# Two of four norm tiles on VectorE: a state-space layer and its experts on one core

## The chip, the cores and the metric

One core of a Trainium2 chip runs the whole program in one launch. Its engines work side by side, each through its own list of instructions in order: TensorE (PE) for matmuls, VectorE (DVE), ScalarE (ACT) and GpSimd (POOL) for elementwise work, SyncE (SP) for starting transfers. The metric is the device time of one launch in microseconds; lower is better.

## The reference, cut to what matters

The input is x, 16 sequences of 256 tokens with 128 features. All norms here are plain: mean and variance over the 128 features of a token.

```python
def layer(x):                       # _L0_attn_ref
    x1 = x + mamba(norm(x) * ln1_g + ln1_b)
    h  = norm(x1) * ln2_g + ln2_b                   # second norm of the layer
    return x1 + relu(h @ ffn_w1.T + b1) @ ffn_w2.T + b2

def experts(x):                     # _L0_ffn_ref, 8 experts, all of them dense
    return sum(silu(x @ Wg[e]) * (x @ Wu[e]) @ Wd[e] for e in range(8))

x = norm(x + layer(x))              # this norm stands ahead of the experts
out = norm(x + experts(x))
```

Inside `mamba` are a projection, a causal convolution over four tokens, a SiLU, a scan over the 256 tokens with 16 states for each of 256 channels, a gate and an output projection. The norms carry 1e-5 beside the variance.

## The kernel before, in words

The 4096 tokens are worked on in 8 groups of 512 (two sequences each). A tile of activations is 128 partitions by 512 numbers, seen as four blocks of 128x128: in a norm, the 128 partitions are tokens, and each of the four blocks has its own column of means and variances.

A group passes through these stages, each a Python generator that is advanced step by step:

- `stage_a` normalises the input (norm "a"), transposes it on TensorE (`pxn`), projects it (`pi`), runs the convolution (`stage_conv`: one ScalarE instruction, three VectorE instructions on `hc`, for each of two halves), and makes the scan's inputs (`pd`, `dbc`, `pv`, `dt`, `u`).
- The scan has 32 steps for a group: `decay` (ScalarE, an exponential into `dA`, in PSUM), `inject` (GpSimd, `dBx`), `step` (VectorE's scan instruction, then the product `hC` with C on VectorE, or on GpSimd with the scan's result in `hS`), `add_state` (a sum over states, on GpSimd into `y` or on TensorE into `py`).
- `stage_c` follows a group's scan: the output projection `po`, the sum `x1`, norm "b" into `x1h`, its transpose `ph`, the small feed-forward part (`pf`, `r`, `pff`), the sum `res`, norm "c" into `x2`, its transpose `px`, and the copy `x2T`, with which the experts can begin.
- `up`, `across` and `down` are the experts' matmuls (`pg`, `pu`, `acc`), with a SiLU on ScalarE and a product on VectorE between; `stage_e` ends a group with norm "e" and the store.

Stages of different groups are interleaved: while group 0 is in `stage_c`, group 1 is in its scan and group 2 in `stage_a`; the experts of group 0 then run beside the scan of group 1. The order is written out by hand, in the strings `PRE`, `START` and `TURN`: each letter is one step of one stage (A for `stage_a` and the convolution, C for `stage_c`, s for a scan step on VectorE, p for one with its product on GpSimd, and so on). A step issues its instructions to their engines there and then, and no engine reorders them. Ahead of the first experts, the letter m puts transposes of a constant (`busy`) on TensorE.

A norm has two functions. `norm_stats` (lines 268 to 286) issues four statistics and four aggregations on VectorE, then two small VectorE instructions on 128x4 numbers (`nm`, the negated mean, line 279, and `ve`, the variance plus 1e-5, line 281), then two on GpSimd: the power -1/2 of `ve` (`rs`, line 283) and the product of `nm` and `rs` (`nb`, line 285). `norm_apply` (line 288) then issues four ScalarE instructions, one for each block, that scale by `rs` and add `nb`. `stage_c` calls it twice: at line 582 for `x1h` and at line 630 for `x2`.

Three things around it matter for what follows. The scan's B and C rows are loaded by SyncE, four steps at a time, into two buffers each; a load waits until the last reader of its buffer is done, and what stands behind it on SyncE's queue waits too. The load of the next group's input, `xt` (line 209), is on the same queue. And `dA` has three PSUM banks, `hC` and `dBx` have six buffers each.

Of the kernel before, what the change touches and what calls it, by code (L numbers as in the profile page):

```python
# [8 lines left out]
FP = mybir.dt.float32  # L9
AF = mybir.ActivationFunctionType  # L10
ALU = mybir.AluOpType

P = 128
# [9 lines left out]
NTT = TB // P  # L23
# [15 lines left out]
EPS = 1e-5  # L39
# [90 lines left out]
def kernel(  # L130
# [25 lines left out]
    nc = tc.nc  # L156
# [11 lines left out]
    small = ctx.enter_context(tc.tile_pool(name="small", bufs=4))  # L168
# [17 lines left out]
    def wide(tag, name, bufs, w=TB):  # L186
        return act.tile([P, TB], FP, tag=tag, bufs=bufs, name=name)[:, :w]

    def wides(tag, name, bufs, n, w):
        t = act.tile([P, n * TB], FP, tag=tag, bufs=bufs, name=name)  # L190
        return t[:, : n * w].rearrange("p (n w) -> p n w", n=n)

    def blocks(tag, name, bufs, n):
        return act.tile([P, NTT, DM], FP, tag=tag, bufs=bufs, name=name)[:, :n, :]
# [70 lines left out]
    def as4(t):  # L265
        return t.rearrange("p (c d) -> p c d", d=DM)

    def norm_stats(src, name):

        n = src.shape[1]  # L270
        st = small.tile([P, NTT, 6], FP, tag="st", name=f"st_{name}")
        mv = small.tile([P, NTT, 2], FP, tag="mv", name=f"mv_{name}")
        for c in range(n):
            nc.vector.bn_stats(st[:, c, :], src[:, c, :])
        for c in range(n):
            nc.vector.bn_aggr(mv[:, c, :], st[:, c, :])

        nm = small.tile([P, NTT], FP, tag="nm", name=f"nm_{name}")
        nc.vector.tensor_scalar(nm[:, :n], mv[:, :n, 0], -1.0, None, ALU.mult)
        ve = small.tile([P, NTT], FP, tag="ve", name=f"ve_{name}")  # L280
        nc.vector.tensor_scalar(ve[:, :n], mv[:, :n, 1], EPS, None, ALU.add)  # L281
        rs = small.tile([P, NTT], FP, tag="rs", name=f"rs_{name}")
        nc.gpsimd.tensor_tensor(rs[:, :n], ve[:, :n], mhalf[:, :n], ALU.pow)  # L283
        nb = small.tile([P, NTT], FP, tag="nb", name=f"nb_{name}")
        nc.gpsimd.tensor_tensor(nb[:, :n], nm[:, :n], rs[:, :n], ALU.mult)
        return rs[:, :n], nb[:, :n]

    def norm_apply(src, dst, scale):
        rs, nb = scale
        for c in range(src.shape[1]):  # L290
            nc.scalar.activation(  # L291
                dst[:, c, :], src[:, c, :], AF.Identity, bias=nb[:, c : c + 1], scale=rs[:, c : c + 1]
            )

    def transpose(pt, src):

        for c in range(src.shape[1]):
            nc.tensor.transpose(pt[:, bass.ts(c, P)], src[:, c, :], ident)
# [6 lines left out]
    def take(name, w, more=0):  # L305

        while len(held) >= limit[0] + more or not free or len(free) <= HELD[1] * (limit[0] == HELD[1]):
            yield
            yield
        held.add(name)  # L310
        return grab(name, w)

    def done(name):
        held.remove(name)
        give(name)
# [23 lines left out]
    def stage_a(g):  # L339
        xt = x_tiles[g]  # L340
        s = state[g] = {}
        yield
        scale = norm_stats(xt, f"a{g}")
        yield
        yield
        yield
        xh = wide("xh", f"xh{g}", 2, W[g])
        norm_apply(xt, as4(xh), scale)
        yield
        pt = yield from take(f"pxn{g}", W[g])  # L350
# [165 lines left out]
    def add_state(t, on_pe):  # L516
# [18 lines left out]
        if last:  # L535
            assert s["gated"] >= h
            if ("sum", h) in s:
                nc.tensor.matmul(
                    s["sum", h], lhsT=ident, rhs=y, start=False,
                    stop=h == NH - 1 or sums(g, NH - 1)[0] != name, skip_group_check=True,  # L540
                )
                y = s["sum", h]
            if h == 0:
                s["yt"] = wides("yt", f"yt{g}", 1, NH, W[g])

            engine = nc.vector if y is not s["y", h] else nc.gpsimd
            engine.tensor_tensor(s["yt"][:, h, :], y, s["zg"][:, h, :], ALU.mult)  # L547
            if name in owner and (h == NH - 1 or sums(g, NH - 1)[0] != name):
                give(name)
            if h == NH - 1:  # L550
                launch("C", stage_c(g))


    def stage_c(g):
        s = state[g]
        xt = x_tiles[g]
        xtf = xt.rearrange("p c d -> p (c d)")
        yield
        po = yield from take(f"po{g}", W[g])
        for c in range(W[g] // P):  # L560
            for h in range(NH):
                nc.tensor.matmul(  # L562
                    po[:, bass.ts(c, P)], lhsT=s["yt"][:, h, bass.ts(c, P)], rhs=outw[:, h, :],
                    start=(h == 0), stop=(h == NH - 1),
                )
        yield
        yield
        x1 = wide("x1", f"x1{g}", 1, W[g])
        nc.vector.tensor_add(x1, po, xtf)
        done(f"po{g}")  # L570
        scale = norm_stats(as4(x1), f"b{g}")
        yield
        yield

        res = wide("res", f"res{g}", 1, W[g])
        nc.gpsimd.tensor_tensor(res, x1, xtf, ALU.add)
        nc.gpsimd.tensor_tensor(
            as4(res), as4(res), fb2_bc[:, :].unsqueeze(1).to_broadcast([P, W[g] // P, DM]), ALU.add
        )
        yield  # L580
        xh = wide("xh", f"x1h{g}", 2, W[g])
        norm_apply(as4(x1), as4(xh), scale)
        yield
        pt = yield from take(f"ph{g}", W[g])
        transpose(pt, as4(xh))
        yield
        h2 = wide("h2", f"h2{g}", 1, W[g])
        nc.scalar.activation(h2, pt, AF.Identity, bias=b2_sb[:, 0:1], scale=g2_sb[:, 0:1])
        done(f"ph{g}")
        yield  # L590
        r = wides("r", f"r{g}", 1, NF, W[g])
        po = None

        def second(f, start, stop):
            for c in range(W[g] // P):
                nc.tensor.matmul(  # L596
                    po[:, bass.ts(c, P)], lhsT=r[:, f, bass.ts(c, P)], rhs=w2[:, f, :],
                    start=start and c == 0, stop=stop and c == W[g] // P - 1, skip_group_check=True,
                )


        if g == 0:
            po = yield from take(f"pff{g}", W[g])
        for f in range(NF):
            pf = yield from take(f"pf{g}_{f}", W[g])
            nc.tensor.matmul(pf, lhsT=w1[:, bass.ts(f, P)], rhs=h2, start=True, stop=True)  # L606
            if g == 0 and f > 0:
                second(f - 1, f == 1, False)
            yield
            nc.scalar.activation(r[:, f, :], pf, AF.Relu, bias=fb1_sb[:, f : f + 1])  # L610
            done(f"pf{g}_{f}")
            yield
        if g > 0:
            po = yield from take(f"pff{g}", W[g])
            for f in range(NF - 1):
                second(f, f == 0, False)
                if f == 1:
                    yield
                    yield
        second(NF - 1, False, True)  # L620
        yield
        yield
        nc.vector.tensor_add(res, po, res)
        done(f"pff{g}")
        scale = norm_stats(as4(res), f"c{g}")
        yield
        yield
        yield
        x2 = blocks("x2", f"x2{g}", 2, W[g] // P)
        norm_apply(as4(res), x2, scale)  # L630
        yield
        pt = yield from take(f"px{g}", W[g])
        transpose(pt, x2)
        yield
        x2T = wide("x2T", f"x2T{g}", 2, W[g])
        nc.scalar.copy(x2T, pt)
        done(f"px{g}")
        state[g] = dict(x2=x2, x2T=x2T)
        slices.extend((g, n) for n in range(NJ[g]))
        yield  # L640
# [163 lines left out]
    while at["w"] < sum(NJ) or any(running.values()):  # L804
# [3 lines left out]
        g, k = scans[min(at["a"], len(scans) - 1)]  # L808
# [56 lines left out]
```

## Time and profile before

| | us |
|---|---|
| median of 3 runs | 932.52 (931.58 to 932.66) |
| the profiled execution | 932.79 |
| its span, first to last instruction | 931.0 |

| engine | busy, us | share of the span |
|---|---|---|
| TensorE | 880.1 | 95% |
| VectorE | 713.9 | 77% |
| ScalarE | 710.9 | 76% |
| GpSimd | 717.6 | 77% |

| what | when, us |
|---|---|
| scan of group 0 ends, `po` of group 0 | 93.8 |
| norm "b" of group 0, ScalarE's part | 99.79 to 101.44 |
| norm "c" of group 0, ScalarE's part | 120.36 to 122.01 |
| first expert matmul | 123.15 |
| last scan's work on GpSimd | 712.8 |
| last matmul of the experts | 923.1 |

The profile is one execution, recorded by the hardware. A row of its timeline gives the start in us from the beginning of the span, the length in us, the engine, the line, the instruction, what it writes and reads with the shapes, and how many of the same kind are merged in the row. In brackets is the time for which the engine sat idle before it, and what released it. VectorE's, ScalarE's and GpSimd's shares are averages over stretches of very different kinds: all three are nearly full while scans and experts run side by side, up to 713 us, and nearly free behind that, where TensorE works alone.

### The profile page before, as it was taken

The page shows a single profiled execution, that of the slowest core. Times are in us where ns is not written, and L with a number is a line of the kernel's source. Part 1 is how long each engine was busy: PE and PEld are TensorE (multiplying, and loading weights), DVE is VectorE, ACT ScalarE, POOL GpSimd, SP SyncE. Part 2 cuts the span into 40 slices and gives each one's busy share as a digit, 9 for nine tenths or more (in the row PEclk, how much of TensorE's full clock was granted, in tenths as well). Part 3 has the DMA queues.
Part 4 walks back from the last instruction along what each step waited for, and adds up shares of the span by engine and source line. Part 5 has one row for each costly group of instructions (what it writes and reads, how often), then busy time and mean ns, then how long its engine had stood idle before and what let it go on. Part 6 is the DMA issues. An engine that isn't in the chain of part 4 may idle for free. (4 is left out here: it accounts for less than half of the span.)

```text
span 931.0 us, 8901 instructions
## 1 busy us (share of the span) xinstructions
PE 880.1 (95%) x2520; PEld 421.2 (45%) x2520; DVE 713.9 (77%) x1144; ACT 710.9 (76%) x995; POOL 717.6 (77%) x637
## 2 busy tenths in 40 slices
PE   5878797999999999999999999999999999999996
PEld 2333443445444543445344543454344544455564
DVE  5699875676989889988988998988898899723222
ACT  5834588888899799989898889979998889533222
POOL 1699999998999887998799879999799979700000
PEclk9799899999999999999999999999999999999999
DMA  7574321121233222222322223221322222000000
GB/s 203 199 236 136 125 71 68 68 103 58 81 102 111 83 90 61 90 90 102 94 80 90 80 94 101 91 94 54 104 90 92 91 79 90 1 1 11 1 0 12
DMA packets 38417, 79.76 MB, mean 86 GB/s; under 512 B 5968, under 2 KB 19168, under 8 KB 38368
## 3 DMA queue, kind: packets, MB, share of 16 engines
q1 hardware_dynamic: 33744, 76.58, 24.6%
q10 hardware_dynamic: 4624, 2.62, 1.0%
q8 instruction: 20, 0.33, 0.1%
q14 instruction: 29, 0.24, 0.1%
HBM read 76.57 MB, written 2.62 MB: 85 GB/s over the span
## 5 line engine op out<-in xcount | busy, mean ns | idle before, releaser
L497 POOL TENSOR_TENSOR dBx<-B,u 128x512 f32<-128x512 f32 x256 | 320.9, 1278 | 17.6 <-DMA B<-bc 17.6
L505 DVE TENSOR_TENSOR_SCAN dA<-dA,dBx 128x512 f32<-128x512 f32 x229 | 279.8, 1222 | 17.5 <-ACT dA L485 14.8
L534 POOL TENSOR_TENSOR y<-y,hC 128x512 f32<-128x512 f32 x223 | 279.6, 1276 | 0.7 <-DVE hC L508 0.6
L652 PE MATMUL pg<-x2T,wg 128*128 128x512 f32 x512 | 253.7, 597 | 7.5 <-ACT h L654 4.8
L661 PE MATMUL pu<-x2T,wu 128*128 128x512 f32 x512 | 250.5, 594 | 4.7 <-ACT h L654 3.3
L679 PE MATMUL acc<-h,wd 128*128 128x512 f32 (+1 forms) x576 | 251.4, 545 | 0.1
L662 DVE TENSOR_TENSOR h<-pu,h 128x512 f32<-128x512 f32 x256 | 170.8, 684 | 104.4 <-PE pu L661 101.4
L654 ACT ACTIVATE h<-pg 128x512 f32<-128x512 f32 x256 | 147.1, 597 | 113.8 <-PE pg L652 111.9
L485 ACT ACTIVATE dA<-dt,A 128x512 f32<-128x512 f32 x256 | 169.5, 685 | 42.1 <-DVE hC L508 34.8
L508 DVE TENSOR_TENSOR hC<-dA,C 128x512 f32<-128x512 f32 x229 | 158.3, 691 | 19.4 <-POOL y L534 4.4
L679 PEld LDWEIGHTS acc<-h,wd 128*128 128x128 f32 x576 | 107.5, 191 | 110.3 <-issue 100.0
L661 PEld LDWEIGHTS pu<-x2T,wu 128*128 128x128 f32 x512 | 95.7, 190 | 124.6 <-issue 90.2
L652 PEld LDWEIGHTS pg<-x2T,wg 128*128 128x128 f32 x512 | 93.8, 190 | 122.6 <-issue 82.7
L485 ACT ACT_TABLE_LOAD x91 | 116.8, 1283 | 2.4 <-ACT x L291 0.5
L654 ACT ACT_TABLE_LOAD x90 | 115.5, 1283 | 3.3 <-ACT dbc L377 1.8
L283 POOL TENSOR_TENSOR rs_e<-ve_e,mhalf 128x4 f32<-128x4 f32 (+1 forms) x9 | 8.5, 946 | 123.3 <-DVE ve_e L281 123.3
L532 PE MATMUL py<-hC,ident 128*128 128x512 f32 x66 | 39.3, 698 | 11.9 <-DVE hC L508 8.0
L505 DVE TENSOR_TENSOR_SCAN hS<-dA,dBx 128x512 f32<-128x512 f32 x27 | 32.3, 1211 | 13.2 <-POOL hC L508 7.2
L449 DVE SCALAR_TENSOR_TENSOR hc<-pi,cw,hc 128x510 f32<-128x510 f32 (+2 forms) x48 | 35.5, 744 | 5.2 <-ACT hc L442 4.0
L508 POOL TENSOR_TENSOR hC<-hS,C 128x512 f32<-128x512 f32 x27 | 34.4, 1277 | 5.4 <-issue 3.0
L596 PEld LDWEIGHTS pff<-w,r 128*128 128x128 f32 x256 | 31.5, 193 | 9.4 <-issue 6.2
L596 PE MATMUL pff<-w,r 128*128 128x128 f32 x256 | 32.1, 278 | 0.9 <-ACT r L610 0.9
(92 smaller groups left out, 595.9 us busy)
## 6 DMA issues: line engine op xcount, KB each, us to landing
B<-bc SPq DMA_DIRECT2D x63, 512.0 KB, 3.9
C<-bc SPq DMA_DIRECT2D x63, 512.0 KB, 4.3
xt<-in_x_dram SPq DMA_DIRECT2D x8, 256.0 KB, 4.4
wg<-in_Wg_dram SPq DMA_DIRECT2D x8, 256.0 KB, 5.7
wu<-in_Wu_dram SPq DMA_DIRECT2D x8, 256.0 KB, 5.6
wd<-in_Wd_dram SPq DMA_DIRECT2D x8, 256.0 KB, 5.4
out_dram<-x ACTq DMA_DIRECT2D x7, 256.0 KB, 4.1
bc<-dbc ACTq DMA_DIRECT2D x8, 64.0 KB, 2.2
```

Of the source, the lines that this page charges most:

```text
L485: nc.scalar.activation(s["dA", k], s["dt"][:, h, :], AF.Exp, scale=A_sb[:, h, n : n + 1])
L497: nc.gpsimd.tensor_tensor(s["dBx", k], s["B", k // NL][:, n % NC, :], s["u"][:, h, :], ALU.mult)
L505: nc.vector.tensor_tensor_scan(to, dA, s.pop(("dBx", k)), 0.0, ALU.mult, ALU.add)
L508: engine.tensor_tensor(hC, to, s["C", k // NL][:, k // NH % NC, :], ALU.mult)
L532: nc.tensor.matmul(s["sum", h], lhsT=ident, rhs=hC, start=first, stop=False, skip_group_check=True)
L534: nc.gpsimd.tensor_tensor(y, y, hC, ALU.add)
L596: nc.tensor.matmul(po[:, bass.ts(c, P)], lhsT=r[:, f, bass.ts(c, P)], rhs=w2[:, f, :], start=start and c == 0, stop=stop and c == W[g] // ...
L652: nc.tensor.matmul(pg[:, cols], lhsT=wg[:, e, bass.ts(f, P)], rhs=s["x2T"], start=True, stop=True)
L654: nc.scalar.activation(s["h", j], pg, AF.Silu)
L661: nc.tensor.matmul(pu[:, cols], lhsT=wu[:, e, bass.ts(f, P)], rhs=s["x2T"], start=True, stop=True)
L662: nc.vector.tensor_mul(s["h", j], pu, s["h", j])
L679: nc.tensor.matmul(acc, lhsT=wd[:, e, f, :], rhs=h[:, cols][:, bass.ts(part, acc.shape[1])], start=(e == 0 and f == 0), stop=(e == NE - 1 ...
```

## The change

In the two norms of `stage_c`, for group 0 alone, blocks 0 and 1 stay on ScalarE, and blocks 2 and 3 go to VectorE as `tensor_scalar` instructions with two scalars read per partition (multiply by `rs`, add `nb`). Their place in VectorE's order follows from where `stage_c` issues them. For `x1h` they come behind the scan instruction into `hS` at 98.28 us and ahead of the one at 99.42 us; for `x2`, behind the six convolution instructions of group 2 at 118.85 us and ahead of the scan at 123.28 us. GpSimd's, TensorE's and SyncE's orders are what they were. In every norm of all groups, `ve` is now issued ahead of `nm`.

```diff
         for c in range(n):
             nc.vector.bn_aggr(mv[:, c, :], st[:, c, :])
+        ve = small.tile([P, NTT], FP, tag="ve", name=f"ve_{name}")
+        nc.vector.tensor_scalar(ve[:, :n], mv[:, :n, 1], EPS, None, ALU.add)
 
         nm = small.tile([P, NTT], FP, tag="nm", name=f"nm_{name}")
         nc.vector.tensor_scalar(nm[:, :n], mv[:, :n, 0], -1.0, None, ALU.mult)
-        ve = small.tile([P, NTT], FP, tag="ve", name=f"ve_{name}")
-        nc.vector.tensor_scalar(ve[:, :n], mv[:, :n, 1], EPS, None, ALU.add)
         rs = small.tile([P, NTT], FP, tag="rs", name=f"rs_{name}")
         nc.gpsimd.tensor_tensor(rs[:, :n], ve[:, :n], mhalf[:, :n], ALU.pow)
...
-    def norm_apply(src, dst, scale):
+    def norm_apply(src, dst, scale, both=False):
+
         rs, nb = scale
-        for c in range(src.shape[1]):
-            nc.scalar.activation(
-                dst[:, c, :], src[:, c, :], AF.Identity, bias=nb[:, c : c + 1], scale=rs[:, c : c + 1]
-            )
+        n = src.shape[1]
+        for c in range(n):
+            s1, s2 = rs[:, c : c + 1], nb[:, c : c + 1]
+            if both and c >= n // 2:
+                nc.vector.tensor_scalar(dst[:, c, :], src[:, c, :], s1, s2, ALU.mult, ALU.add)
+            else:
+                nc.scalar.activation(dst[:, c, :], src[:, c, :], AF.Identity, bias=s2, scale=s1)
...
         xh = wide("xh", f"x1h{g}", 2, W[g])
-        norm_apply(as4(x1), as4(xh), scale)
+        norm_apply(as4(x1), as4(xh), scale, g == 0)
...
         x2 = blocks("x2", f"x2{g}", 2, W[g] // P)
-        norm_apply(as4(res), x2, scale)
+        norm_apply(as4(res), x2, scale, g == 0)
```

## The prediction

> **What bounds the kernel now.** I read the page first: the span in slices, then the chain that ended last; then the waits, and the timeline from 92 to 160 us, where the change acts. The chain lists nothing before 665.69 us, so what the handover at 93 to 126 us is worth at the end has to be read from TensorE's row and its waits.
>
> ```profile
> PE   5878797999999999999999999999999999999996
> ...
> 149.83 1.12 PE L652 MATMUL pg<-x2T,wg 128*128 128x512 f32 x2 [2.28 <-ACT h L654]
> 172.76 1.12 PE L661 MATMUL pu<-x2T,wu 128*128 128x512 f32 x2 [1.09 <-DVE h L662]
> ```
>
> A slice is 23.3 us. TensorE is loosely filled up to about 123 us, when the first expert matmul can run, and is full from there to the end. The stretches 123 to 140, 180 to 200 and 616 to 665 us show it busy for 16.6 of 17, 20.0 of 20 and 48.9 of 49 us. So the end is the start of the experts plus a nearly fixed amount of TensorE work; only the waits between 140 and 173 us (0.31, 2.28, 2.42 and 1.09 us) could swallow a delay. The start of the experts is set here:
>
> ```profile
> 99.42 1.20 DVE L505 TENSOR_TENSOR_SCAN dA<-dA,dBx 128x512 f32<-128x512 f32 x1
> 99.70 1.27 POOL L508 TENSOR_TENSOR hC<-hS,C 128x512 f32<-128x512 f32 x1
> 99.79 1.65 ACT L291 ACTIVATE x1h<-x,nb_b,rs_b 128x128 f32<-128x128 f32 x4 [2.89 <-POOL nb_b L285]
> ...
> 101.41 0.32 SPq L472 DMA_DIRECT2D C<-bc  x1
> 101.78 0.43 SPq L209 DMA_DIRECT2D xt<-in_x_dram  x1
> 102.00 0.78 ACT L588 ACTIVATE h<-ph,b,g 128x512 f32<-128x512 f32 x1 [0.56 <-PE ph L298]
> ...
> 106.20 0.87 DVE L274 BATCH_NORM_STATS2 st_a<-xt 128x6 f32<-128x128 f32 x4 [2.99 <-DMA xt<-in_x_dram]
> ...
> 107.18 1.27 POOL L497 TENSOR_TENSOR dBx<-B,u 128x512 f32<-128x512 f32 x1
> 107.38 1.09 DVE L279 TENSOR_SCALAR nm_a<-mv_a 128x4 f32<-128x4 f32 x1
> 108.39 1.30 DVE L281 TENSOR_SCALAR ve_a<-mv_a 128x4 f32<-128x4 f32 x1
> 108.40 1.27 POOL L534 TENSOR_TENSOR y<-y,hC 128x512 f32<-128x512 f32 x1
> ...
> 118.85 4.51 DVE L449 SCALAR_TENSOR_TENSOR hc<-pi,cw,hc 128x510 f32<-128x510 f32 x6
> ...
> 120.36 1.65 ACT L291 ACTIVATE x<-res,nb_c,rs_c 128x128 f32<-128x128 f32 x4
> ...
> 122.52 0.57 ACT L636 COPY x2T<-px 128x512 f32<-128x512 f32 x1
> 122.74 1.28 POOL L534 TENSOR_TENSOR y<-y,hC 128x512 f32<-128x512 f32 x1
> 123.15 1.98 PE L652 MATMUL pg<-x2T,wg 128*128 128x512 f32 x4 [0.33 <-ACT x2T L636]
> ```
>
> To be seen: ScalarE is idle for 2.89 us before x1h and four tiles take it 1.65 us, so there is something to share. But VectorE, the engine that is to take half, runs without a gap from 109.61 to 124.4 us, and the six convolution instructions of group 2 stand in it while ScalarE does the second norm.
>
> **Part 1, variance first.** The two 128x4 instructions start 0.07 us apart (98.14 and 98.21), so swapped, the power on GpSimd starts 0.07 us earlier in each norm. Off TensorE's path that is nothing: the experts' matmuls cover it (after 140 us GpSimd itself waits 13.8 and 22.4 us in all for the variances of the b and c norms). On the path lies the last norm alone, at 926 us: -0.07 us.
>
> **Part 2, the first norm (x1h).** ScalarE gives up two of four tiles, 2 x 0.39 us. VectorE gets two tensor_scalar of 128x128 behind the scan of 98.28, ahead of the scan of 99.42, and waits for nb (99.68 after part 1). No row has a 128x128 tensor_scalar. By the nearest, the 128x4 at 0.17 us and the 128x32 at 0.198 us, I estimate 0.25 us. The Trainium skill (VectorE: DVE Perf Modes, the perf-mode tier table) gives fp32 tensor_scalar two elements per cycle, which with the formula of the page's errata section, 58 + 64 cycles, makes an estimate of 0.13 us; part 2 would then save about 0.5 us. Against it stands what the rows at 107.38 show: two 128x4 took 1.09 and 1.30 us, and each ended 0.02 us after a running GpSimd instruction (108.45, 109.67). The same skill says why (SBUF — State Buffer, Who interferes with whom): this form uses a port pair that is GpSimd's too, and the second to come is blocked for the whole of the other's instruction. At 425.84 us, with GpSimd idle, the same instruction took 0.17 us. I take the rows. Here GpSimd starts hC right behind nb, at 99.63, and then res (100.92). So the first tile ends near 101.05. For the second the rows disagree: at 108.4 it waited for one more GpSimd instruction, at 212.56 it slipped in:
>
> ```profile
> 212.35 0.30 DVE L279 TENSOR_SCALAR nm_a<-mv_a 128x4 f32<-128x4 f32 x1
> 212.56 0.16 DVE L281 TENSOR_SCALAR ve_a<-mv_a 128x4 f32<-128x4 f32 x1
> 212.58 2.50 POOL L497 TENSOR_TENSOR dBx<-B,u 128x512 f32<-128x512 f32 x2
> ```
>
> So the last tile ends at 101.2 (early) or 102.3 (late), against 101.44 before: h at 102.00 moves by -0.3 or +0.9 us. Queued behind it on VectorE is the scan of 99.42, which moves by +1.7 or +2.9; behind that the product hC at 100.66, whose end frees the C buffer. SP's load of C (101.41) waits for that, and the load of xt (101.78) stands behind it on the same queue. So st_a, for which VectorE sat idle 2.99 us, moves along, to 107.9 or 109.06. Here some comes back. Early, ve_a still meets y on GpSimd and ends at about 109.65, as before: 0. Late, it gets there at 110.25, y is over, nothing blocks, and it ends at 110.4 in place of 109.69: +0.75. Everything up to 119 us (VectorE has no gap, GpSimd and ScalarE follow its norm) carries 0 or +0.75. Without any block two tiles cost VectorE 0.6 us, and ve_a still ends at 109.7: 0.
>
> **Part 3, the second norm (x2).** On ScalarE it ran at 120.36 to 122.01. Its two VectorE tiles stand in VectorE's order behind the six convolutions (to 123.36) and ahead of the scan of 123.28. So they start at 123.3 (early) or 124.05 (late). GpSimd is then in the y of 122.74 (to 124.02 or 124.7); after it GpSimd waits for that very scan, so only one block is paid. The last tile ends at 124.2 or 124.95, against 122.01. x2T follows 0.5 us later, at 124.65 or 125.45: +2.1 or +2.9 us. ScalarE's two saved tiles are worth nothing, since it then waits at x2T, with the table load, the silus and all it does up to 154.7 us behind it. The first pg moves by the same.
>
> **Part 4, the clock.** TensorE has nothing but four transposes from about 122 us to the new x2T. The rule of the skill (TensorE: Matmul & The Clock Gate, Why this matters for your kernels) asks for gaps under about 3 us; this gap, with two transposes in it, would about pass. The windows say that less is enough: transposes and a 0.85 us wait in 112 to 115 us were followed by half clock (the third number from the end of a row is the granted clock; 116 to 118 us has 0.50).
>
> ```profile
> 112.00:114.00 2.00, 1.33 (x5) 0.55 (x4) 1.90 (x3) 2.00 (x5) 2.00 (x3) 1.00 0.00 0
> 114.00:116.00 2.00, 1.64 (x9) 1.65 (x10) 1.91 (x3) 1.55 (x3) 1.99 (x2) 0.74 0.67 231
> ```
>
> By the rule nothing is added; by the rows 3.4 us at half clock fall on the first pg, which costs TensorE up to 1.7 us, 1.4 of it ahead of pd (126.69). ScalarE, busy without a gap, would have reached dbc 0.45 us after pd's old pace, so the chain pd, dbc, pv, dt takes +0.95. I take the rows: +3.1 (early) or +3.85 (late) for ScalarE and TensorE. GpSimd's product at 132.01, behind the scan of 130.07, which is behind the second h (129.47), moves by 2.85 or 3.6.
>
> **The sum.** From 136.5 to 154.7 us ScalarE has no gap, so it hands its shift to TensorE at the waits of 149.83 and 154.23; the wait at 172.76 goes back to GpSimd's y, moved by 2.85 or 3.6, and takes off some 0.2. Later waits are all for results that TensorE's own work fed. So +3.0 or +3.7; between the two rows that disagree I take the middle, +3.3. With -0.07: 932.79 (the profiled execution; its span of 931.0 and 1.8 around it) + 3.2 = 936.0. That execution lies 0.27 above the median of 932.52, so I predict 935.7.
>
> **The rivals.**
> 1. Blocked, but the clock stays up: +1.5 (early: GpSimd's chain +1.45, TensorE's +2.1) to +2.9 (late): 934.0 to 935.4. For it: the wait is under 3 us. Against: the rows of 112 to 118. Chance 0.18.
> 2. GpSimd doesn't block a tensor_scalar whose scalars are read per partition; no row has that form. Then part 2 is 0 and part 3 is two tiles of 0.2 us behind the convolutions: x2T +1.6, end +1.0 to +1.6: 933.5 to 934.1. Chance 0.08.
> 3. The other side, not slower: the start of the experts is late, but the waits of 140 to 173 us (6.1 us in all) take it in, and the end stays: 932.4. It decides at 136.5 us: if ScalarE's run up to 154.7 starts less than about 0.4 us late, the waits at 149.83 and 154.23 shrink by what TensorE lost. Against it: ScalarE stands in order at x2T, and has only 1.21 + 0.26 + 0.26 us of waits up to there, all for TensorE, which is late as well. Chance 0.07.
> 4. VectorE loses more than one turn per tile to GpSimd: one more GpSimd instruction (1.27 us) in each norm and a longer stand at half clock, +5: 937.5. Chance 0.05.
>
> **How the numbers follow.** The forecast's case has 0.62: 935.0 to 936.6 by its own two ends and the spread of the runs. The range 933.7 to 937.6 leaves out rival 3, a part of rival 2 and half of rival 4, 0.13 in all. 0.2% is 1.9 us, about what a measurement of this kernel can tell from no change; above 934.4 counts as slower. Same: 0.04 of rival 1 (its lower end), 0.08 of rival 2, 0.05 of rival 3: 0.17. Faster: 0.02 of rival 3. Slower: 0.81.
>
> **What would show it.** In the new profile: x1h and x2 on VectorE with about 1.2 us a piece where GpSimd is busy, ending with a GpSimd instruction; xt loaded later by what x1h costs; x2 behind the six convolutions; the first pg at 125.3 to 126.1; half clock behind it; and from 180 us on every row later by about 3 us. I am wrong if pg starts before 124 us, or if it starts late and the rows at 180 us are not.

## The result, and the profile after

| | before | after |
|---|---|---|
| median, us | 932.52 (5 runs, 931.03 to 932.66) | 936.12 (5 runs, 935.55 to 936.85) |
| the profiled execution, us | 932.79 | 936.01 |
| its span, us | 931.0 | 934.2 |
| mean granted clock | 0.985 | 0.981 |

The ratio is 1.0039, with a 95% interval of 1.0027 to 1.0051: slower by 3.6 us (2.5 to 4.8).

TensorE's row of the slices after, against the one shown of before (40 slices of 23.4 us, each digit the busy share in tenths): full from the eighth slice, at 163 us, in both.

```profile
PE   5778787999999999999999999999999999999996
```

One thing has to be known before two profiles are laid side by side. In after's, norm "b" of group 0 starts 1.5 us earlier than in before's (`rs_b` at 96.93 against 98.45 us). Most of that, 1.1 us, arises at 24 to 31 us: at 24 to 26 us the granted clock was 0.50 in before's execution and 1.00 in after's. So what the change did is read as a distance from `rs_b` in the same profile:

| us behind the start of `rs_b` | before | after | shift |
|---|---|---|---|
| `x1h`, last tile ends | 2.99 | 3.82 | +0.83 |
| load of `xt` issued | 3.33 | 6.12 | +2.79 |
| `st_a` starts | 7.75 | 10.70 | +2.95 |
| `rs_a` starts | 11.33 | 12.14 | +0.81 |
| first `hc` on VectorE | 20.40 | 21.29 | +0.89 |
| `x2`, last tile ends | 23.56 | 26.69 | +3.13 |
| `x2T` starts | 24.07 | 27.26 | +3.19 |
| first `pg` (length) | 24.70 (1.98) | 27.90 (3.21) | +3.20 |
| `pd` starts | 28.24 | 32.67 | +4.43 |
| `dbc` starts | 30.64 | 34.58 | +3.94 |

The timeline of after in the first norm (start, length, engine, line, instruction; in brackets the idle time before it and its releaser):

```profile
98.18 1.27 POOL L512 TENSOR_TENSOR hC<-hS,C 128x512 f32<-128x512 f32 x1
98.27 0.88 ACT L297 ACTIVATE x1h<-x,nb_b,rs_b 128x128 f32<-128x128 f32 x2 [2.82 <-POOL nb_b L285]
98.27 2.48 DVE L295 TENSOR_SCALAR x1h<-x,rs_b,nb_b 128x128 f32<-128x128 f32 x2 [0.22 <-POOL nb_b L285]
...
99.41 1.26 POOL L580 TENSOR_TENSOR res<-x,xt 128x512 f32<-128x512 f32 x1
...
100.67 1.22 DVE L509 TENSOR_TENSOR_SCAN dA<-dA,dBx 128x512 f32<-128x512 f32 x1
...
100.81 0.48 PE L302 MATMUL ph<-ident,x1h 128*128 128x128 f32 x1 [0.90 <-DVE x1h L295]
...
102.68 0.32 SPq L476 DMA_DIRECT2D C<-bc  x1
...
103.05 0.43 SPq L209 DMA_DIRECT2D xt<-in_x_dram  x1
...
107.63 0.87 DVE L274 BATCH_NORM_STATS2 st_a<-xt 128x6 f32<-128x128 f32 x4 [3.15 <-DMA xt<-in_x_dram]
...
108.82 0.17 DVE L278 TENSOR_SCALAR ve_a<-mv_a 128x4 f32<-128x4 f32 x1
108.90 0.16 DVE L281 TENSOR_SCALAR nm_a<-mv_a 128x4 f32<-128x4 f32 x1
```

To be seen: ScalarE's pair is done in 0.88 us, VectorE's takes 2.48, and ends at 100.75, just behind GpSimd's two instructions (98.18 to 99.45, 99.41 to 100.67). The scan stands behind it, then the C load, then `xt` on the same queue, then `st_a`. At 108.82 the two small instructions take 0.17 and 0.16 us where before they took 1.09 and 1.30: that is what comes back.

The second norm, and the start of the experts:

```profile
118.22 4.52 DVE L453 SCALAR_TENSOR_TENSOR hc<-pi,cw,hc 128x510 f32<-128x510 f32 x6
...
119.65 0.88 ACT L297 ACTIVATE x<-res,nb_c,rs_c 128x128 f32<-128x128 f32 x2 [1.65 <-POOL nb_c L285]
...
120.20 0.86 PE L302 MATMUL px<-ident,x 128*128 128x128 f32 x2 [1.73 <-ACT x L297]
...
122.01 1.27 POOL L538 TENSOR_TENSOR y<-y,hC 128x512 f32<-128x512 f32 x1
122.65 0.97 DVE L295 TENSOR_SCALAR x<-res,rs_c,nb_c 128x128 f32<-128x128 f32 x2
...
123.42 0.73 PE L302 MATMUL px<-ident,x 128*128 128x128 f32 x2 [2.36 <-DVE x L295]
...
124.19 0.59 ACT L640 COPY x2T<-px 128x512 f32<-128x512 f32 x1 [3.08 <-PE px L302]
...
124.83 3.21 PE L656 MATMUL pg<-x2T,wg 128*128 128x512 f32 x4
```

ScalarE has its half at 120.53. VectorE begins the other at 122.65, when the six convolutions are through, and TensorE and ScalarE stand for 2.36 and 3.08 us. The windows show the clock over this stretch (behind the length, the busy time of TensorE comes first; the granted clock is the third number from the end):

```profile
118.00:120.00 2.00, 0.47 (x4) 0.23 (x3) 1.90 (x6) 0.35 (x2) 1.60 (x3) 1.00 0.01 2
120.00:122.00 2.00, 0.81 (x2) 0.32 (x2) 1.93 (x4) 1.11 (x3) 2.00 (x2) 0.63 0.00 0
122.00:124.00 2.00, 0.58 (x3) 0.50 (x4) 2.00 (x4) 0.00 (x0) 1.28 (x2) 0.50 0.00 0
124.00:126.00 2.00, 2.00 (x7) 1.26 (x6) 1.90 (x3) 1.79 (x2) 1.10 (x1) 0.50 0.00 0
126.00:128.00 2.00, 2.00 (x5) 0.82 (x4) 0.67 (x1) 1.72 (x4) 2.00 (x3) 0.67 0.00 0
```

The 0.63 of 120 to 122 us is 1.00 for half a microsecond and 0.50 for the rest: half clock began at about 120.5 us. That is behind the wait of 1.73 us for ScalarE's half, and ahead of the wait of 2.36 us, which runs from 121.06.

And the two waits that the prediction had named as the place where ScalarE hands on its shift, with what follows them in TensorE's timeline:

```profile
152.74 1.13 PE L656 MATMUL pg<-x2T,wg 128*128 128x512 f32 x2 [2.28 <-ACT h L658]
...
157.14 1.20 PE L665 MATMUL pu<-x2T,wu 128*128 128x512 f32 x2 [2.42 <-ACT h L658]
158.13 1.92 PE L656 MATMUL pg<-x2T,wg 128*128 128x512 f32 x2
159.84 1.84 PE L427 MATMUL pz<-xn,inw 128*128 128x512 f32 x2
...
173.53 3.84 PE L665 MATMUL pu<-x2T,wu 128*128 128x512 f32 x8
```

The waits of 2.28 and 2.42 us are as long as before, to the hundredth, and both stand 2.91 us later on the clock of the profile, 4.4 later behind `rs_b`. The two rows at 158.13 and 159.84 ran at half clock (1.92 and 1.84 us, where before's took 1.02 each): +1.7. The wait of 1.09 us before a `pu` at 172.76 is gone: -1.1. So 4.4 + 1.7 - 1.1 = 5.0 behind `rs_b`; less the 1.5 us by which this execution was ahead, 3.5, where the rows from 177 us on are 3.5 later and the span is 3.2 longer.

### The profile page after: what moved, and what is told of

The parts are those of the page before. It is cut to its first block, busy times and chain, and to the rows that moved or that the text cites. A ratio compares the mean times of both kernels' runs of the same rounds, so it can differ in the third digit from the quotient of the medians.

```text
span 934.2 us, 8917 instructions
## 1 busy us (share of the span) xinstructions
PE 879.6 (94%) x2520; PEld 422.5 (45%) x2520; DVE 715.5 (77%) x1148; ACT 709.6 (76%) x991; POOL 717.8 (77%) x637
```

## The experiments

All times are against runs of the kernel before on the same chip. "us later" is the ratio less one, times 932 us, with its 95% interval. Four questions: what each part is worth alone, whether GpSimd's block or the place in VectorE's order is the cost of part 3, whether a late start of the experts reaches the end, and what the clock adds.

**Each part alone.** Of after, the second of these edits makes `x1h_only`, the first `x2_only`, and both `variance_first`:

```diff
-        norm_apply(as4(x1), as4(xh), scale, g == 0)
+        norm_apply(as4(x1), as4(xh), scale)
...
-        norm_apply(as4(res), x2, scale, g == 0)
+        norm_apply(as4(res), x2, scale)
```

> Only the first of the two norms (x1h) is shared with VectorE; x2 stays whole on ScalarE; variance first everywhere. My theory (blocked at x1h, most of it regained because st_a waits for its load anyway): x1h's pair takes about 2.5 us on VectorE, ve_a behind it is no longer blocked, the convolutions and x2T come 0.7 to 0.8 us late against their distance from nb_b, and the end moves by +0.7 us (933.2). Rival, the block at x1h is the whole loss and nothing is regained: VectorE stays 2.7 us late up to the convolutions, end +2.7 us or more (935.3). Rival, sharing x1h pays and only x2 costs: end -0.3 us (932.2).

> Only the second norm (x2) is shared; x1h stays whole on ScalarE; variance first everywhere. My theory: VectorE reaches x2's two tiles behind the six convolutions, x2T comes 2.1 us later than before, TensorE stands idle for most of that and falls to half clock under the first pg; end +2.1 to +3.1 us (934.6 to 935.6). Rival, the block at x1h is the whole loss: end within 0.6 us of before. Rival, a late start of the experts is taken in by TensorE's waits at 140 to 173 us: x2T late by 2.1 us, end within 0.6 us of before.

> Variance first in all norms, nothing on VectorE that was not there before. My theory: 0.07 us off the last norm, no difference that can be measured (932.4). Rival, it works in each of the 32 norms: 32 x 0.07 = -2.2 us (930.3).

Measured: `x1h_only` 933.83, 1.0014 (1.0007 to 1.0022), 1.3 us later (0.7 to 2.1). `x2_only` 934.84, 1.0033 (1.0021 to 1.0044), 3.1 later (2.0 to 4.1). `variance_first` 931.69, 0.9999 (0.9989 to 1.0008), which is no difference. So most of the loss hangs on the second norm, and the first costs a little more than the 0.75 of the sum: in its profile `x2T` is 0.6 late, the wait of 1.73 us ahead of the transposes is there too, and the four passes of the first `pg` take 2.94 us at half clock, so `pd` is 1.5 late. The two parts add to 4.4 where the whole gave 3.6; the intervals allow the same.

**GpSimd's block.** VectorE's two tiles read PSUM in place of SBUF: a copy of 0.42 us puts that half of `x1` and of `res` in the bank of `po` or `pff`, which is given back after the norm.

```diff
+        if g == 0:
+            nc.vector.tensor_copy(po[:, 2 * P :], x1[:, 2 * P :])
...
-                nc.vector.tensor_scalar(dst[:, c, :], src[:, c, :], s1, s2, ALU.mult, ALU.add)
+                nc.vector.tensor_scalar(dst[:, c, :], other[:, c, :], s1, s2, ALU.mult, ALU.add)
```

> The changed kernel, but the two VectorE tiles of each norm are read from a copy in PSUM, which VectorE writes right behind nm (one more instruction of 128x256 in each of the two norms, about 0.4 us, off the way to rs). Place and order of the tiles are as in the changed kernel. My theory (GpSimd blocks a tensor_scalar that reads and writes SBUF, and not one that reads PSUM): each pair takes about 0.4 to 0.5 us, whatever GpSimd does; st_a's load goes out 1.5 us earlier than in the changed kernel; x2's tiles start right behind the convolutions and x2T comes about 2.0 us later than before, where the changed kernel has 3.1; end +1.6 to +2.9 us (934.1 to 935.4). Rival, the long x1h pair is not a matter of SBUF ports (a slow start with per-partition scalars, say): the pair stays near 2.5 us and the end near 936.1.

Measured: 936.38, 1.0048 (1.0035 to 1.0060), 4.5 us later (3.3 to 5.6). The expectation of the end was missed. The timeline of this kernel:

```profile
100.09 0.70 DVE L295 TENSOR_SCALAR x1h<-po,rs_b,nb_b 128x128 f32<-128x128 f32 x2
100.31 1.27 POOL L512 TENSOR_TENSOR hC<-hS,C 128x512 f32<-128x512 f32 x1 [0.28 <-issue]
...
119.81 4.52 DVE L453 SCALAR_TENSOR_TENSOR hc<-pi,cw,hc 128x510 f32<-128x510 f32 x6
...
122.26 0.41 PE L302 MATMUL px<-ident,x 128*128 128x128 f32 x2 [2.53 <-DVE hc L453]
...
124.25 0.72 DVE L295 TENSOR_SCALAR x<-pff,rs_c,nb_c 128x128 f32<-128x128 f32 x2
```

The pairs took 0.70 and 0.72 us, beside a running GpSimd in the first case, in place of 2.48 and 0.97. So it is the block that made the first pair long: rival 2, a form that GpSimd does not block, falls for operands in SBUF. But the second pair still begins behind the six convolutions, `x2T` is 2.73 late, half clock falls on `pg` again (3.76 us), and `pd` is where it was in after (32.76 against 32.67). The end of this run is not that of the block alone: with `pff`'s bank held, `px` was given a bank that the convolutions were still reading, and TensorE's first two transposes waited 2.53 us for them, where in after they ran at 120.20. In part 3 the block is some 0.5 us, by which `x2T` came earlier than in after; what is left, 2.7, is the place in the order and the 0.7 us by which the convolutions were late already.

**The place in the order.** The same two tiles of `x2`, from SBUF, between the third and the fourth of the six convolutions; `x1h` all on ScalarE.

```diff
+        if g == 2 and h == 1:
+            later.pop()()
...
+        if g == 0:
+            later.append(lambda: norm_apply(as4(res), x2, scale, "dve"))
...
-        norm_apply(as4(res), x2, scale, g == 0)
+        norm_apply(as4(res), x2, scale, "act" if g == 0 else False)
```

> Only x2 is shared, as in x2_only, but its two VectorE tiles stand between the first three and the last three convolution instructions, not behind all six. My theory (the place behind the convolutions is what makes the experts late): the tiles end 1.5 to 2.7 us after nb_c in place of 3.9, x2T starts at 23.7 to 24.9 us after the start of rs_b (24.0 in variance_first, 25.2 in x2_only, with VectorE 1.2 us ahead there), and the end is -0.3 to +1.5 us against before (932.0 to 933.8). Rival, the block by GpSimd at x2 costs most of it: x2T stays at 25 us or later and the end at +2.5 us (934.8).

Measured: 932.98, 1.0008 (0.9998 to 1.0018), 0.7 us later (-0.2 to 1.7).

```profile
117.58 1.27 POOL L543 TENSOR_TENSOR y<-y,hC 128x512 f32<-128x512 f32 x1
...
118.45 1.70 DVE L297 TENSOR_SCALAR x<-res,rs_c,nb_c 128x128 f32<-128x128 f32 x2
...
118.80 1.27 POOL L506 TENSOR_TENSOR dBx<-B,u 128x512 f32<-128x512 f32 x1
...
121.36 3.00 PE L663 MATMUL pg<-x2T,wg 128*128 128x512 f32 x4
```

Each tile ended with a GpSimd instruction once more, 1.70 us for both, and still `x2T` came at 23.74 behind `rs_b`, ahead of before's 24.07. In this execution VectorE was 1.15 us ahead at the convolutions (19.25 behind `rs_b`, against 20.40), so the fair measure is `x2_only`, where it was at 19.25 too: against that, with the place alone changed, `x2T` came 1.5 earlier, `pd` 1.2, and the end is 0.7 us later than before's in place of 3.1, with the intervals apart by a little. The `pg` behind it took 3.00 us at half clock, so `pd` was 0.7 later than before's all the same.

A variant joined both ideas, the pair from PSUM between the second and the third convolution (`x2_early_psum`, the copy of `from_psum` and the insertion of `between_convs`).

> A version that might gain: only x2 is shared; its two VectorE tiles are read from a copy in PSUM (so GpSimd can't block them) and stand behind the second convolution instruction, where nb_c has just come. My theory: the pair takes 0.7 us and ends with ScalarE's pair or 0.3 us behind it; x2T comes up to 0.5 us earlier than in variance_first, end -0.5 us to 0 against variance_first, which these rounds can't tell from no change. Rival, the 0.4 us copy and the later convolutions eat it: x2T no earlier, silu of the convolution late, end +0.5 us.

Measured: 934.15, 1.0020 (1.0012 to 1.0027), 1.9 us later. A miss, by a cause outside the question: the pair was through at 119.95, but with `pff`'s bank held, `px` was given a bank that the convolution was still reading, and TensorE waited for it:

```profile
119.23 0.72 DVE L297 TENSOR_SCALAR x<-pff,rs_c,nb_c 128x128 f32<-128x128 f32 x2
...
120.75 1.09 PE L304 MATMUL px<-ident,x 128*128 128x128 f32 x4 [3.04 <-DVE hc L458]
```

**A late start alone.** The kernel before, with three ScalarE copies of `r` ahead of group 0's `x2T`, and nothing of the change:

```diff
+        if g == 0:
+            for f in range(3):
+                nc.scalar.activation(r[:, f, :], r[:, f, :], AF.Identity)
```

> The kernel before, with three more ScalarE instructions of 128x512 right ahead of group 0's x2T (they copy a tile of the feed-forward part that nobody reads any more onto itself; about 1.9 us), so that the experts start late and nothing else is changed. My theory (the end follows the start of the experts one for one, and half clock under the first pg adds up to 1 us): x2T +1.9 us, end +1.9 to +3.0 us (934.2 to 935.3). Rival, TensorE's waits at 140 to 173 us take it in: end within 0.6 us of before (932.3).

Measured: 934.81, 1.0024 (1.0015 to 1.0034), 2.2 us later (1.4 to 3.2), with `x2T` 1.57 late.

```profile
124.08 0.56 ACT L639 COPY x2T<-px 128x512 f32<-128x512 f32 x1
...
124.70 3.04 PE L655 MATMUL pg<-x2T,wg 128*128 128x512 f32 x4 [1.88 <-ACT x2T L639]
```

A late start of the experts reaches the end, so rival 3, which had all of it absorbed, falls. In this profile half clock came again under `pg`, from about 125.5 us, behind the wait of 1.88 us: `pd` is 3.25 late and the span 2.6 longer. That the end moved by more than the start did is shown by this profile, not by the interval, which holds the 1.57 too.

**The clock.** Matmuls on constants (`fill`, 128x512 each) keep TensorE busy around the transposes of `x2`: in after (`clock_kept`), in `between_convs` (`between_clock`, the same edit), and three of them behind the transposes in `late_x2T` (`late_clock`).

```diff
+    def fill(n):
+        t = bank("acc", "fill")
+        for _ in range(n):
+            nc.tensor.matmul(t, lhsT=ident, rhs=w1, start=True, stop=True, skip_group_check=True)
...
-        transpose(pt, x2)
+        if g == 0:
+            fill(2)
+            for c in range(2):
+                nc.tensor.transpose(pt[:, bass.ts(c, P)], x2[:, c, :], ident)
+            fill(2)
+            for c in range(2, 4):
+                nc.tensor.transpose(pt[:, bass.ts(c, P)], x2[:, c, :], ident)
+        else:
+            transpose(pt, x2)
```

> The changed kernel, with two matmuls of 128x512 on TensorE ahead of the first transpose into px and two more between the second and the third, into a bank that nobody reads, so that TensorE is busy while it would wait for x2. My theory (half clock under the first pg is about a third of the loss): granted clock 1.0 from the first pg to pd, the four passes of pg take 2.0 us and not 3.2, pd starts 1.0 to 1.7 us closer to pg than in the changed kernel, end 934.6 to 935.4. Rival, the clock has no part in it because ScalarE sets the pace there: end unchanged at 936.1.

> The kernel of between_convs (x2's tiles 2 and 3 on VectorE between its convolutions, x1h all on ScalarE), and four matmuls on constants between the transposes of x2, as in clock_kept. Theory (position and clock are the two costs, the split itself is none): the first pg takes about 2.0 us in place of 3.0, x2T stays at 23.7 us after the start of rs_b, pd comes at about 27.8, 0.4 ahead of before's 28.2, and the time is 0.1 to 0.6 us below before's, 931.5 to 932.2. Rival (the waits of 140 to 173 us take such a small gain in, as they are set by ScalarE): the time is before's within 0.3 us. Rival 2 (the clock is not what between_convs lost): still 0.9 above before's.

> The kernel of late_x2T (nothing of the change; three ScalarE copies of 0.55 us ahead of the experts of group 0, x2T 1.57 us late, end 2.3 to 2.7 us late) and three matmuls on constants behind the transposes of x2. Theory (a late start passes to the end at its own size, the half clock under the first pg adds the rest): pg takes about 2.0 us, pd is 1.6 to 1.9 late in place of 3.25, and the end 1.3 to 1.8 later than before's. Rival (the clock's loss is taken in by later waits, and the lateness of x2T alone gives the end): 2.3 to 2.7 later, as without the matmuls.

The timeline and one window of `clock_kept` (its profile is of a long execution, 936.88 against the median of 933.61; it holds 6.8 us of half clock from 155.4 us on):

```profile
123.60 1.88 PE L307 MATMUL fill<-w,ident 128*128 128x512 f32 x4
126.29 0.58 PE L648 MATMUL px<-ident,x 128*128 128x128 f32 x2 [0.80 <-DVE x L295]
126.71 0.60 PE L804 MATMUL busy<-ident 128*128 128x128 f32 x4
127.54 1.98 PE L669 MATMUL pg<-x2T,wg 128*128 128x512 f32 x4 [0.24 <-ACT x2T L653]
```

```profile
125.00:127.00 2.00, 1.20 (x7) 0.60 (x6) 2.00 (x4) 0.09 (x1) 1.15 (x1) 1.00 0.00 0
```

The first `pg` is back at 1.98 us with a clock of 1.00, in all three kernels (1.98, 1.99, 1.88). Us later than before, without and with the matmuls, and the shift of `pd` behind `rs_b`:

| | end without | end with | `pd` without | `pd` with |
|---|---|---|---|---|
| after, `clock_kept` | 3.6 (2.5 to 4.8) | 1.2 (0.5 to 2.1) | +4.4 | +3.0 |
| `late_x2T`, `late_clock` | 2.2 (1.4 to 3.2) | 1.1 (0.3 to 2.0) | +3.25 | +2.25 |
| `between_convs`, `between_clock` | 0.7 (-0.2 to 1.7) | -0.1 (-0.9 to 0.8) | +0.7 | +0.4 |

Ratios with the matmuls: 1.0013 (1.0005 to 1.0022), 1.0012 (1.0003 to 1.0021) and 0.9999 (0.9990 to 1.0009). In each pair the end is nearer to before's with them; the intervals of the first pair are apart, those of the others overlap. I had counted the matmuls too short: two of 128x512 take 1.9 us and three 2.7, so in `late_clock` they held `pg` back by 0.8 us, and in `between_clock` the last transposes by 0.9. That is why `pd` missed its 27.8 there (28.67). `between_clock` is level with before; what a shorter filling could still win, 0.8 us, is within the interval of these runs, and it was not tried. No version measured here is faster than before.

## Why the prediction was right

The time was predicted as 935.7 and came as 936.1. The mechanism held in the main; that the number fits so well is luck, as sizes in its sum were off and cancel.

**Part 1** was not contradicted: `variance_first` shows no difference at the end, with an interval far wider than the 0.07 us in question.

**Part 2** took the block from rows of 128x4 instructions and left two cases open. The late one came: the last tile at 102.27 (102.3 predicted) and `st_a` at 109.15 (109.06), both counted from before's `rs_b`, `ve_a` unblocked, and the convolutions 0.8 to 0.9 late (0.75). The price that spoke for the change, an estimate of 0.13 us a tile from the Trainium skill (VectorE: DVE Perf Modes, the perf-mode tier table and the errata section), was far off. The second tile of after's second norm, from SBUF, began when GpSimd's `y` had just ended (123.28 us) and took 0.34 us, more than the 0.25 I had estimated; one from PSUM took 0.38 to 0.40.

```profile
123.29 0.34 DVE L295 TENSOR_SCALAR x<-res,rs_c,nb_c 128x128 f32<-128x128 f32 x1
```

**Part 3** held: `x2` behind the six convolutions, one block paid, `x2T` +3.2 (2.9). `between_convs` against `x2_only` shows that it is the place more than the block.

**Part 4** took the rows and not the rule, and half clock came. Its place and length were not foreseen: 6.8 us in place of 3.4, and from about 120.5 us, behind a wait of 1.73 us that the prediction did not have. Both waits, 1.73 and 2.36 us, are under the 3 us that the Trainium skill gives (TensorE: Matmul & The Clock Gate, Why this matters for your kernels). The late second norm is not the only way to it: `x1h_only`, with `x2` whole on ScalarE, has the wait of 1.73 us and half clock under `pg` as well. The first `pg` came at 126.35, counted from before's `rs_b`, a little later than the 125.3 to 126.1 that I had named. Rival 1, the clock staying up, is what `clock_kept` made by force: 933.6, a little below the 934.0 to 935.4 that I had for it. Rival 4's further lost turns are not in the profile of after. `pd` shifted by 4.4 (4.3 predicted) and `dbc` by 3.9 (3.85).

**The sum** cancels its errors. How much later than in before's profile TensorE reaches the same matmuls shows where:

| us later than in before's profile | `rs_b` | `acc` at 131.26 | `acc` at 173.72 | span |
|---|---|---|---|---|
| after | -1.5 | +2.9 | +3.5 | +3.2 |
| `from_psum` | +0.3 | +4.8 | +4.2 | +4.0 |
| `late_x2T` | 0.0 | +3.2 | +2.6 | +2.6 |
| `clock_kept` | +1.4 | +4.4 | +5.0 | +4.1 |
| `late_clock` | +0.3 | +2.6 | +3.0 | +1.9 |
| `x2_only` | -1.4 | +0.5 | +1.2 | +0.7 |
| `variance_first` | -1.2 | -1.3 | -1.2 | -2.6 |

- TensorE carried `pd`'s shift of 4.4 on, as the second column shows for after (2.9 and 1.5). I had let 3.85, the shift of `dbc`, stand for both engines: 0.6 too little.
- The half clock at 158 us, 1.7 us, was not in the sum. The profiles of `x1h_only`, `x2_only`, `between_convs`, `clock_kept`, `between_clock` and `late_clock` have such a stretch beginning at 152 to 157 us; those of before, `variance_first`, `from_psum`, `x2_early_psum` and `late_x2T` have none.
- The wait at 172.76 took in 1.1, where I had counted 0.2. It takes in 1.1 in each profile with that half clock ahead of it, and 0.6 in the late ones without. So much of rival 3 is true, and no more: the lag at 131 us stands to a few hundredths up to 150 us. Behind 174 us another 0 to 1.4 us come off, but no less in `variance_first`, which has no late start, than in the others, so that is not lateness taken in.
- The 1.5 us by which this execution was ahead at `rs_b` was not in the sum either.

The late case alone, 3.7, would have given 936.15. I took the middle of two rows that disagreed, and the runs chose the later.

**Open.** I set the clock at 0.95 us on the chain to the end. After against `clock_kept` makes it 1.4 at `pd` and 2.4 in the medians, where the intervals leave 0.4 to 4.3. With `pd` 3.0 late, `clock_kept` is only 1.2 later in the median of its executions. Its profile does not show that lateness taken in, 4.4 at 131 us and 4.1 at the end, but it is of one of its two longest executions, with `rs_b` 1.4 late; `x2_only`'s is of its shortest. So how a median comes about is not shown by one profile of a kernel. That after was 1.5 us ahead at `rs_b` is seen in most, not all, of the profiles with the variance first; whether that is more than chance was not tried.

## What to carry to other kernels

Half of an engine's work, moved to a second engine, comes back when that engine's order and the instructions of GpSimd beside it let it, not when its instruction would be done: look first at what stands ahead of the new place, and at what GpSimd runs beside it. A gap ahead of a long run of matmuls cost twice here, once as a wait and once as half clock behind it, so cost both, and look for the waits further ahead as well. Lay two profiles side by side from a common event near the change, not from the start of the span.

## What the hardware showed that was not expected

The same meeting on VectorE goes one way or the other. In `x2_only` and in `variance_first`, which are the same program up to here, the same two instructions meet the same GpSimd instructions:

```profile
106.04 0.99 DVE L278 TENSOR_SCALAR ve_a<-mv_a 128x4 f32<-128x4 f32 x1
106.94 0.16 DVE L281 TENSOR_SCALAR nm_a<-mv_a 128x4 f32<-128x4 f32 x1
106.96 1.27 POOL L538 TENSOR_TENSOR y<-y,hC 128x512 f32<-128x512 f32 x1
```

```profile
106.22 1.04 DVE L278 TENSOR_SCALAR ve_a<-mv_a 128x4 f32<-128x4 f32 x1
107.18 1.31 DVE L281 TENSOR_SCALAR nm_a<-mv_a 128x4 f32<-128x4 f32 x1
107.20 1.26 POOL L538 TENSOR_TENSOR y<-y,hC 128x512 f32<-128x512 f32 x1
```

In the first, `nm_a` slipped in between two GpSimd instructions and took 0.16 us; in the second it waited through the next one, 1.31 us. Both times the start is recorded 0.02 us ahead of GpSimd's, so the rows do not show what decides. The first kernel's VectorE was 1.2 us ahead from there (`hc` 19.25 us behind `rs_b`, against 20.42).

And half clock came behind shorter waits than I had thought even from the rows: in `between_convs` waits of 1.08 and 0.89 us stood around the transposes of `x2`, the granted clock fell at about 120.0 us, inside the second (0.51 from 120 to 121 us), and the first `pg` ran at half clock (3.00 us).
